# Carry by 128 channels, a second buffer and a later normalisation in a state-space scan on GpSimd and VectorE

## The chip, the cores and the metric

The kernel runs on one core of one Trainium2 chip. The metric is the device time of one execution in microseconds; the median of the runs is compared. Engine names in the profile: PE is TensorE (PEld its weight loads), DVE VectorE, ACT ScalarE, POOL GpSimd, SP SyncE; SPq is SyncE's queue, from which every DMA of the stage is issued.

## The reference

A network of two layers on x of shape 4 x 128 x 64 x 64, in fp32. Layer 0 (convolutions, an ordering of patches and a scan with 16 states) is not touched. Layer 1 takes the 4096 tokens of each batch (128 features), normalises them, and adds this scan with 256 states for each of 256 channels:

```
x_proj = x @ W_in;  xs, z = split(x_proj)
delta = xs @ W_delta;  Bv = xs @ W_B;  Cv = xs @ W_C
state = exp(delta_t[d] * A[d, n]) * state + delta_t[d] * B_t[n] * xs_t[n]
y_t[d] = sum over n of state[d, n] * C_t[n]
out = (y * silu(z)) @ W_out
```

The n-th state is fed by the n-th channel of xs, so B times xs is one vector over n, called `u` in the kernel. After a second normalisation the layer adds a spectral filter: sixteen causal convolutions over all 4096 tokens, each followed by a 128 x 128 matrix, two versions of each (for the sequence and for the sequence with alternating signs), and three short taps.

## The kernel before

Layer 1 is one loop over 8192 steps in an order written out by hand. A part is a chunk of 512 tokens of one batch: 4 batches x 8 chunks are 32 parts of 256 steps, and step d of a part does channel d for all 256 states (two halves of 128 partitions) and 512 tokens. `normalise`, `project`, `output`, `fetch`, `carry`, `spread`, `lift`, `scan`, `contract` and `put` are functions inside `layer1`.

What is issued at step k, in this order:

- `fetch` (L1068), every second step: one DMA `dlb<-delta` (L1071) brings the deltas of channels k+8 and k+9, 512 tokens each, to all partitions. Four such buffers.
- `carry` (L1074): in parts after a batch's first chunk, two GpSimd instructions (L1079, L1080) multiply the factors of the first token, `af`, by the states kept in `last`, and add the result to the first values `vf`. Now 32 channels at a time, six steps ahead of the first of them.
- `spread` (L1082), every second step, four ahead: one GpSimd instruction (L1085) multiplies `u` by the deltas of two channels for tokens 1 to 511 and both halves, 2044 elements per partition, into one of three buffers `v`; a small ScalarE copy (L1089) puts the first token's `vf` beside it.
- `lift` (L1092), one ahead: two ScalarE activations (L1094) write exp(delta A) into one of two PSUM buffers `da`.
- jobs that are due (`later`), then one piece of the block product's work: after each eight channels, `contract` (L1102) splits into six pieces: TensorE products `yp` (L1114), the ScalarE copies `ye` of `put` (L1120) with a DMA `yd<-ye` (L1121), and the copy to `last` (L1125).
- `scan` (L1096): one VectorE instruction (L1097), 1024 elements, reading `da` and `v`.
- a piece of the side work `beside(n)`: `output` of the part before, then `project` of the part after. Both are generators that yield "mm" (taken at step 6 of each eight), "post" (step 7) or "free" (the next step). Each contains one `normalise` (L744): statistics on VectorE, two small ScalarE instructions, a power and a product on GpSimd (L759, L760), then four ScalarE activations (L764). The last piece of `project` is the Exp of `af`. The last of `output` stores `x3` and, for every second chunk, hands over a block of 1024 tokens to the spectral filter.
- at step 7 of each eight, `fetch_y` issues four or eight small DMAs `yt<-yd` (L1137).
- matrix products of the spectral filter, `conv` (L1045) and `fin` (L989), as many columns as a step's credit allows (1.4 x 512 at first, 1.7 x 512 from the middle of the third batch). Their inputs are loaded up to three products ahead by `load` (L948): `pq` (L956, five buffers) and `strip` (L962, three buffers), by SyncE. What is left when the steps are over is issued after the loop.

Every engine executes its own instructions in that order, and so does SyncE's queue: a DMA that waits for a buffer holds all DMAs behind it.

Of the kernel before, what the change touches and what calls it, by code (L numbers as in the profile page):

```python
# [8 lines left out]
F32 = mybir.dt.float32  # L9
# [588 lines left out]
GD = 8  # L598
# [78 lines left out]
def layer1(ctx: ExitStack, tc, ident, half, w_in, w_delta, w_b, w_c, w_out, a_t, phi, pqd, mud, x2, x3, out):  # L677
# [20 lines left out]
    wk = ctx.enter_context(tc.tile_pool(name="s_wk", bufs=2))  # L698
    sp = ctx.enter_context(tc.tile_pool(name="s_sp", bufs=3))
# [44 lines left out]
    def normalise(t):  # L744

        st = sm.tile([128, NT, 6], F32, tag="st", name="st")
        mv = sm.tile([128, NT, 2], F32, tag="mv", name="mv")
        for i in range(NT):
            nc.vector.bn_stats(st[:, i, :], t[:, i, :])
        for i in range(NT):  # L750
            nc.vector.bn_aggr(mv[:, i, :], st[:, i, :])
        yield "free"
        ve = sm.tile([128, NT], F32, tag="ve", name="ve")
        nc.scalar.activation(ve, mv[:, :, 1], AF.Identity, bias=eps)
        ms = sm.tile([128, NT], F32, tag="ms", name="ms")
        nc.scalar.activation(ms, mv[:, :, 0], AF.Copy, scale=-1.0)
        yield "free"
        rs = sm.tile([128, NT], F32, tag="rs", name="rs")
        nc.gpsimd.tensor_tensor(rs, ve, half[:, :NT], ALU.pow)  # L759
        nc.gpsimd.tensor_tensor(ms, ms, rs, ALU.mult)  # L760
        yield "free"
        yield "free"
        for i in range(NT):
            nc.scalar.activation(  # L764
                t[:, i, :], t[:, i, :], AF.Identity, bias=ms[:, i : i + 1], scale=rs[:, i : i + 1]
            )
# [11 lines left out]
    def project(b, ch, into):  # L778
# [12 lines left out]
        yield "free"  # L791
        tr = tr.rearrange("p (i c) -> p i c", i=NT)
        yield from normalise(tr)
        yield "mm"
        ps = middle()
# [152 lines left out]
    def load(i):  # L948

        (b, blk, sources, _, _), r, k, side, src = queue[i]
        if src == sources[0]:
            segs = (0, 2) if blk == 0 else (min(blk + 1, 3), 1)
            pq = sp.tile([128, 2, 128], F32, tag="pq", name="pq", bufs=5)
            nc.sync.dma_start(pq[:, 0 : segs[1]], pqd[k, side][:, bass.ds(*segs)])  # L956
            mats[i] = pq
        lo = max(0, 512 * (blk - src) - 384)
        width = 896 if src < blk else 512
        strip = sp.tile([128, 896], F32, tag="strip", name="strip")  # L960
        start = (NK + k) * row + r if side else k * row + 1
        nc.sync.dma_start(strip[:, :width], bass.AP(phi.tensor, start + lo, [[1, 128], [1, width]]))  # L962
        strips[i] = strip, lo

    def products():
# [50 lines left out]
        while True:  # L1016
# [15 lines left out]
            while issued < len(queue) and issued < i + 3:  # L1032
                load(issued)
                issued += 1
# [33 lines left out]
    def fetch(d, ready):  # L1068

        dl = wk.tile([128, VD, TS], F32, tag="dlb", name="dlb", bufs=4)  # L1070
        nc.sync.dma_start(dl, ready[3][bass.ds(d, VD), :].partition_broadcast(128))  # L1071
        return dl

    def carry(ch, d, ready):  # L1074

        af, vf = ready[4:]
        cols = bass.ds(d, 32)
        if ch:
            nc.gpsimd.tensor_tensor(af[:, :, cols], af[:, :, cols], last[:, :, cols], ALU.mult)  # L1079
            nc.gpsimd.tensor_tensor(vf[:, :, cols], vf[:, :, cols], af[:, :, cols], ALU.add)  # L1080

    def spread(d, dl, ready):  # L1082

        v = wk.tile([128, VD, 2, TS], F32, tag="v", name="v", bufs=3)
        nc.gpsimd.tensor_tensor(  # L1085
            v[:, :, :, 1:], ready[0][:, :, 1:].unsqueeze(1).broadcast_to((128, VD, 2, TS - 1)),
            dl[:, :, 1:].unsqueeze(2).broadcast_to((128, VD, 2, TS - 1)), ALU.mult,
        )
        nc.scalar.copy(v[:, :, :, 0], ready[5][:, :, bass.ds(d, VD)].rearrange("p h d -> p d h"))  # L1089
        return v  # L1090

    def lift(d, da, dl):  # L1092
        for h in range(2):
            nc.scalar.activation(da[:, h, 1:], dl[:, d % VD, 1:], AF.Exp, scale=at[:, h, d : d + 1])  # L1094

    def scan(d, s, v, da):  # L1096
        nc.vector.tensor_tensor_scan(  # L1097
            s[:, d % GD].rearrange("p h t -> p (h t)"), da.rearrange("p h t -> p (h t)"),
            v[:, d % VD].rearrange("p h t -> p (h t)"), 0.0, ALU.mult, ALU.add,
        )  # L1100

    def contract(s, c, g, keep):  # L1102


        yd = dr.tile([130, NT, 32, GD], F32, tag="yd", name="yd", bufs=12)
        yp = {}

        def products(i):
            if i % 2 == 0:
                yp[i // 2] = pm.tile([128, 2, GD, 32], F32, tag="mm", name="yp")  # L1110
            for h in range(2):
                for q in range(4):
                    t = bass.ds(128 * i + 32 * q, 32)
                    nc.tensor.matmul(  # L1114
                        yp[i // 2][bass.ts(q, 32), i % 2], c[:, h, t], s[:, :, h, t], start=h == 0, stop=h == 1
                    )

        def put(j):
            ye = wk.tile([128, 2, 32, GD], F32, tag="ye", name="ye", bufs=1)
            nc.scalar.copy(ye, yp[j].rearrange("p i d t -> p i t d"))  # L1120
            nc.sync.dma_start(yd[0:128, 2 * j : 2 * j + 2], ye)  # L1121

        def carried():
            if keep:
                nc.scalar.copy(  # L1125
                    last[:, :, bass.ts(g, GD)].rearrange("p h d -> p d h"), s[:, :, :, TS - 1]
                )

        def take(yt):

            flat = yd.rearrange("p i t d -> (p i t d)")
            for q in range(4):
                rows = flat[bass.ds(32 * q * NT * 32 * GD, 32 * (NT * 32 + 1) * GD)]
                rows = rows.rearrange("(r x) -> r x", r=32)[:, 0 : NT * 32 * GD].rearrange(
                    "r (i y) -> r i y", i=NT
                )[:, :, 0:GD]
                nc.sync.dma_start(yt[bass.ts(q, 32), :, bass.ts(g, GD)], rows)  # L1137

        return [
            lambda: products(0), lambda: products(1), lambda: put(0), lambda: products(2),  # L1140
            lambda: (products(3), carried()), lambda: put(1),
        ], take

    def due():
        for job in [j for j in later if j[0] <= now[0]]:
            later.remove(job)
            job[2]()
# [6 lines left out]
    steps = 256 * len(parts)  # L1154
# [5 lines left out]
    def beside(n):  # L1160

        if n:
            yield from output(*parts[n - 1], done.pop(n - 1), ready.pop(n - 1)[2])
        if n + 1 < len(parts):
            ready[n + 1] = tiles()
            yield from project(*parts[n + 1], ready[n + 1])
# [9 lines left out]
                    done[m] = big.tile([128, NT, 256], F32, tag="yt", name="yt", bufs=1)  # L1176
                take(done[m])

    for k in range(-8, steps):
        now[0] = k  # L1180
        j = k + 8
        if 0 <= j < steps and j % VD == 0:
            dls[j // VD] = fetch(j % 256, ready[j // 256])
        j = k + 6
        if 0 <= j < steps and j % 32 == 0:
            carry(parts[j // 256][1], j % 256, ready[j // 256])
        j = k + 4
        if 0 <= j < steps and j % VD == 0:
            vs[j // VD] = spread(j % 256, dls[j // VD], ready[j // 256])
        j = k + 1  # L1190
        if 0 <= j < steps:
            lift(j % 256, factors[j % 2], dls[j // VD])
        if k < 0:
            continue
        due()
        n, d = divmod(k, 256)
        b, ch = parts[n]
        if pieces:
            pieces.pop(0)()
        if d % GD == 0:  # L1200
            s = wk.tile([128, GD, 2, TS], F32, tag="s", name="s")
        scan(d, s, vs[k // VD], factors[k % 2])
        if d % GD == GD - 1:
            more, take = contract(s, ready[n][1], d // GD, ch + 1 < NCH)
            pieces += more
            takes.append((n, take))
        if d == GD:
            side = beside(n)
            kind = next(side, None)
        at_step = d % GD  # L1210
        if kind == "free" or (kind == "mm" and at_step == 6) or (kind == "post" and at_step == 7):
            kind = next(side, None)
        if at_step == GD - 1:
            fetch_y(n, d)
        pace = 1.4 if n < 5 * NCH // 2 else 1.7
        credit = min(credit + pace * TS, pace * TS)
        while credit > 0:
            cost = next(spectral)
            if cost == 0:
                break  # L1220
            credit -= cost
# [93 lines left out]
```

## Time and profile before

| | us |
|---|---|
| median of 3 runs | 22132.84 (22130.33 to 22134.94) |
| the profiled execution's own time | 22129.28 |
| its span, first to last instruction | 22127.6 |
| VectorE busy | 20448.7 (92%) |
| GpSimd busy | 20181.7 (91%) |
| TensorE busy (matmuls) | 17758.9 (80%) |
| ScalarE busy | 15725.0 (71%) |

The span holds layer 0 and the weights of the spectral filter (up to about 3140 us), the 256-state stage (first spread at 3142.1, last scan at 21771.5) and a rest in which the spectral filter ends. A row of a group gives line, engine, operation, the tiles written and read, count, then the busy time and the mean duration in ns, then the engine's idle time just before these instructions and what ended it. A row of waits gives who waited for whom, us in total, times and the longest. A row of a timeline gives the start and the length in us.

### The profile page before, as it was taken

The page shows a single profiled execution, that of the slowest core. Times are in us where ns is not written, and L with a number is a line of the kernel's source. Part 1 is how long each engine was busy: PE and PEld are TensorE (multiplying, and loading weights), DVE is VectorE, ACT ScalarE, POOL GpSimd, SP SyncE. Part 2 cuts the span into 40 slices and gives each one's busy share as a digit, 9 for nine tenths or more (in the row PEclk, how much of TensorE's full clock was granted, in tenths as well). Part 3 has the DMA queues.
Part 4 walks back from the last instruction along what each step waited for, and adds up shares of the span by engine and source line. Part 5 has one row for each costly group of instructions (what it writes and reads, how often), then busy time and mean ns, then how long its engine had stood idle before and what let it go on. Part 6 is the DMA issues. An engine that isn't in the chain of part 4 may idle for free.

```text
span 22127.6 us, 292872 instructions
## 1 busy us (share of the span) xinstructions
PE 17758.9 (80%) x99156; PEld 7777.4 (35%) x99156; DVE 20448.7 (92%) x11842; ACT 15725.0 (71%) x28971; POOL 20181.7 (91%) x5932
## 2 busy tenths in 40 slices
PE   8788844474867888886858888869598899999999
PEld 4444421131323333342323333324233344434344
DVE  3588879999999999999999999999999999999993
ACT  0477747777777777777777777777777777777773
POOL 0477759999999999999999999999999999999993
PEclk9899976686988999997979999979699999999999
DMA  0255544464656776675656777757577677777775
GB/s 27 78 139 140 140 136 151 150 198 151 206 186 200 218 222 218 218 220 180 213 173 217 220 219 218 220 179 229 164 225 222 216 233 233 232 230 230 230 226 154
DMA packets 2399971, 4238.15 MB, mean 192 GB/s; under 512 B 778200, under 2 KB 1235968, under 8 KB 2395136
## 3 DMA queue, kind: packets, MB, share of 16 engines
q1 hardware_dynamic: 2398464, 4219.40, 62.0%
q8 instruction: 781, 12.80, 0.2%
q14 instruction: 726, 5.95, 0.1%
HBM read 3600.52 MB, written 617.88 MB: 191 GB/s over the span
## 4 chain that ended last, share of the span: by engine, by line
DVE 49%; POOL 17%; PE 14%; ACT 9%; issue 6%; DMA 4%; SPq 0%; DVEq 0%; POOLq 0%; ACTq 0%
DVE s L1097 43%; POOL v L1085 16%; ACT da L1094 6%; PE conv L1045 6%; DVE states L493 3%; PE conv L96 2%; DMA yd<-ye 2%; PE yp L1114 2%; DVE p L497 2%; PE fin L989 1%; ACT f L485 1%; PE y L509 1%; PE mm L402 0%; ACT t L764 0%; ACT ye L1120 0%
## 5 line engine op out<-in xcount | busy, mean ns | idle before, releaser
L1085 POOL TENSOR_TENSOR v<-u,dlb 128x2044 f32<-128x2044 f32 x4096 | 18343.1, 4522 | 111.5 <-DMA dlb<-delta 93.7
L1097 DVE TENSOR_TENSOR_SCAN s<-da,v 128x1024 f32<-128x1024 f32 x8192 | 18056.5, 2270 | 383.3 <-ACT da L1094 315.7
L1094 ACT ACTIVATE da<-dlb,at 128x511 f32<-128x511 f32 x16384 | 11299.4, 690 | 2062.9 <-DVE s L1097 1598.3
L1045 PE MATMUL conv<-strip,tok 128*128 128x512 f32 (+3 forms) x20480 | 8646.5, 552 | 3.9 <-DMA strip<-in_phi 3.8
L1114 PE MATMUL yp<-s,c 128*32 128x256 f32 x65536 | 5015.4, 437 | 2972.2 <-DVE s L1097 1617.2
L1045 PEld LDWEIGHTS conv<-strip,tok 128*128 128x128 f32 x20480 | 3689.4, 192 | 4132.0 <-issue 3754.7
L1114 PEld LDWEIGHTS yp<-s,c 128*32 128x32 f32 x65536 | 1987.9, 121 | 6755.1 <-issue 1831.8
L1089 ACT COPY v<-vf 128x4 f32<-128x4 f32 x4096 | 813.4, 199 | 2260.8 <-DVE s L1097 2142.4
L471 POOL TENSOR_TENSOR v<-dx,bcb 128x1024 f32<-128x1024 f32 x512 | 1207.2, 2358 | 433.4 <-DVE states L493 427.9
L989 PE MATMUL fin<-conved,pq 128*128 128x512 f32 (+1 forms) x3200 | 1423.1, 540 | 13.5 <-ACT conved L1056 4.2
L493 DVE TENSOR_TENSOR_SCAN states<-f,v 128x1024 f32<-128x1024 f32 x512 | 1176.0, 2297 | 172.5 <-ACT f L485 123.3
L1120 ACT COPY ye<-yp 128x512 f32<-128x512 f32 x2048 | 1186.1, 579 | 148.9 <-DMA yd<-ye 132.2
L485 ACT ACTIVATE f<-dt,an 128x255 f32<-128x255 f32 x2048 | 973.4, 476 | 418.7 <-DVE states L493 368.0
L509 PE MATMUL y<-p,ident 128*128 128x512 f32 x2048 | 1005.1, 619 | 149.4 <-DVE p L497 144.4
L1056 ACT COPY conved<-conv 128x512 f32<-128x512 f32 x1344 | 778.2, 579 | 338.3 <-PE conv L1045 336.8
L497 DVE TENSOR_TENSOR p<-states,bcb 128x1024 f32<-128x1024 f32 x512 | 627.1, 1225 | 41.1 <-DVE states L493 2.7
L989 PEld LDWEIGHTS fin<-conved,pq 128*128 128x128 f32 x3200 | 532.0, 194 | 226.0 <-issue 164.1
L509 PEld LDWEIGHTS y<-p,ident 128*128 128x128 f32 x2048 | 368.4, 195 | 680.4 <-issue 355.2
L127 POOL TENSOR_TENSOR rs<-sq,half 128x1 f32<-128x1 f32 x4 | 2.2, 560 | 485.2 <-DVE sq L125 485.2
L402 PE MATMUL mm<-ow,yg 128*32 128x128 f32 x2048 | 283.2, 298 | 106.8 <-ACT om L406 105.3
L402 PEld LDWEIGHTS mm<-ow,yg 128*32 128x32 f32 x2048 | 236.8, 139 | 213.6 <-ACT om L406 128.4
L1005 DVE TENSOR_TENSOR xo<-xo,fin 128x512 f32<-128x512 f32 x32 | 21.3, 665 | 300.8 <-PE fin L997 300.8
(232 smaller groups left out, 6259.3 us busy)
## 6 DMA issues: line engine op xcount, KB each, us to landing
dlb<-delta SPq DMA_DIRECT2D x4096, 512.0 KB, 4.1
strip<-in_phi SPq DMA_DIRECT2D x1536, 448.0 KB, 4.7
yd<-ye SPq DMA_DIRECT2D x2048, 256.0 KB, 4.0
bcb<-bcd SPq DMA_DIRECT2D x1024, 256.0 KB, 4.2
strip<-in_phi SPq DMA_DIRECT2D x1024, 256.0 KB, 4.3
pq<-pqd SPq DMA_DIRECT2D x1088, 64.0 KB, 3.9
yt<-yd SPq DMA_DIRECT2D x4096, 4.0 KB, 3.3
pq<-pqd SPq DMA_DIRECT2D x256, 128.0 KB, 4.0
```

Of the source, the lines that this page charges most:

```text
L471: nc.gpsimd.tensor_tensor(v, ready[n][2][:, :, bass.ts(i, SUB)].unsqueeze(1).broadcast_to((128, 2, 2, SUB)), bc[:, 0].unsqueeze(2).broadca ...
L485: nc.scalar.activation(factors[j % 2][:, a, k, 1:], ready[n][1][:, k, SUB * i + 1 : SUB * i + SUB], AF.Exp, scale=an[:, k, 2 * g + a : 2 * ...
L493: nc.vector.tensor_tensor_scan(states.rearrange(flat), factors[j % 2].rearrange(flat), v.rearrange(flat), 0.0, ALU.mult, ALU.add)
L497: nc.vector.tensor_tensor(p, states, bc[:, 1].unsqueeze(2).broadcast_to((128, 2, 2, SUB)), ALU.mult)
L509: nc.tensor.matmul(t.rearrange("p k t -> p (k t)"), ident, p[:, a].rearrange("p k t -> p (k t)"), start=g == 0 and a == 0, stop=False, ski ...
L989: nc.tensor.matmul(fin[:, bass.ds(c0, w)], pq[:, n, :], u[:, bass.ds(c0, w)], start=begin and n == 0, stop=end and not partly, skip_group_ ...
L1045: nc.tensor.matmul(ps[:, skip:], tok[:, 1 - r if side else r, j, :], strip[:, bass.ds(c0 - lo, TS - skip)], start=src == sources[0] and j ...
L1085: nc.gpsimd.tensor_tensor(v[:, :, :, 1:], ready[0][:, :, 1:].unsqueeze(1).broadcast_to((128, VD, 2, TS - 1)), dl[:, :, 1:].unsqueeze(2).br ...
L1094: nc.scalar.activation(da[:, h, 1:], dl[:, d % VD, 1:], AF.Exp, scale=at[:, h, d : d + 1])
L1097: nc.vector.tensor_tensor_scan(s[:, d % GD].rearrange("p h t -> p (h t)"), da.rearrange("p h t -> p (h t)"), v[:, d % VD].rearrange("p h t ...
L1114: nc.tensor.matmul(yp[i // 2][bass.ts(q, 32), i % 2], c[:, h, t], s[:, :, h, t], start=h == 0, stop=h == 1)
L1120: nc.scalar.copy(ye, yp[j].rearrange("p i d t -> p i t d"))
```

## The change

Three edits in the 256-state stage. `carry` takes 128 channels in one pair of instructions and is issued ten steps ahead of the first of them; the loop therefore begins two steps earlier. `ye` has the pool's two buffers in place of one, and `pq` four in place of five. In `normalise` five pieces lie between the GpSimd power and the activations, in place of two.

```diff
@@ normalise
         nc.gpsimd.tensor_tensor(rs, ve, half[:, :NT], ALU.pow)
         nc.gpsimd.tensor_tensor(ms, ms, rs, ALU.mult)
-        yield "free"
-        yield "free"
+        for _ in range(5):
+            yield "free"
         for i in range(NT):
@@ load
-            pq = sp.tile([128, 2, 128], F32, tag="pq", name="pq", bufs=5)
+            pq = sp.tile([128, 2, 128], F32, tag="pq", name="pq", bufs=4)
@@ carry
-        cols = bass.ds(d, 32)
+        cols = bass.ds(d, 128)
         if ch:
             nc.gpsimd.tensor_tensor(af[:, :, cols], af[:, :, cols], last[:, :, cols], ALU.mult)
             nc.gpsimd.tensor_tensor(vf[:, :, cols], vf[:, :, cols], af[:, :, cols], ALU.add)
@@ put
-            ye = wk.tile([128, 2, 32, GD], F32, tag="ye", name="ye", bufs=1)
+            ye = wk.tile([128, 2, 32, GD], F32, tag="ye", name="ye")
@@ the loop over steps
-    for k in range(-8, steps):
+    for k in range(-10, steps):
...
-        j = k + 6
-        if 0 <= j < steps and j % 32 == 0:
+        j = k + 10
+        if 0 <= j < steps and j % 128 == 0:
             carry(parts[j // 256][1], j % 256, ready[j // 256])
```

## The prediction

> **What bounds the kernel now.** I read the page's groups of instructions first: two groups of nearly the same size fill two engines.
>
> ```profile
> L1085 POOL TENSOR_TENSOR v<-u,dlb 128x2044 f32<-128x2044 f32 x4096 | 18343.1, 4522 | 111.5 <-DMA dlb<-delta 93.7
> L1097 DVE TENSOR_TENSOR_SCAN s<-da,v 128x1024 f32<-128x1024 f32 x8192 | 18056.5, 2270 | 383.3 <-ACT da L1094 315.7
> ```
>
> A spread on GpSimd serves two scans on VectorE, 4.52 us against 2 x 2.27. So the busy times over the 256-state stage alone decide (the windows view; columns: window, length, then busy us of PE, PEld, DVE, ACT and POOL, clock, DMA share, GB/s):
>
> ```profile
> 3146.00:21774.00 18628.00, 14902.14 (x90440) 6340.33 (x90444) 18243.90 (x9028) 13984.76 (x25818) 18533.51 (x4668) 0.90 0.66 207
> 21774.00:22127.60 353.60, 344.98 (x1060) 179.39 (x1052) 5.29 (x14) 62.31 (x111) 1.22 (x2) 1.00 0.41 116
> ```
>
> GpSimd is busy 18,533.5 of 18,628 us, 99.5%; VectorE has 384 us to spare. The stage is a GpSimd queue with small holes; the last 354 us are TensorE's (345 busy). The waits of the stage, VectorE's, then ScalarE's, then SyncE's queue (total us, times, longest):
>
> ```profile
> DVE s L1097 <- ACT da L1094: 315.7, 173, 5.3
> DVE s L1097 <- POOL v L1085: 58.3, 95, 7.8
> ```
>
> ```profile
> ACT ye L1120 <- DMA yd<-ye: 130.0, 89, 6.2
> ACT v L1089 <- POOL vf L1080: 112.4, 94, 1.4
> ACT t L764 <- POOL ms L760: 110.3, 51, 3.2
> ```
>
> ```profile
> SPq L1071 <- ACT da L1094: 8420.5, 3632, 5.7
> ...
> SPq L962 <- PE conv L1045: 560.4, 458, 4.9
> ```
>
> The reader is to see that ScalarE's three waits (353 us) resemble VectorE's 316 us: ScalarE stalls, the next factor `da` is late, the scan waits. But VectorE catches up, since GpSimd is slower; such a stall costs time only where it reaches GpSimd. It does so by one route, seen in the timeline:
>
> ```profile
> 4404.76 1.65 ACT L764 ACTIVATE t<-t,ms,rs 128x128 f32<-128x128 f32 x4 [2.99 <-POOL ms L760]
> ...
> 4407.81 17.56 DVE L1097 TENSOR_TENSOR_SCAN s<-da,v 128x1024 f32<-128x1024 f32 x8 [3.42 <-ACT da L1094]
> ...
> 4463.64 4.50 POOL L1085 TENSOR_TENSOR v<-u,dlb 128x2044 f32<-128x2044 f32 x1 [4.65 <-DMA dlb<-delta]
> ```
>
> A `dlb` load reuses a buffer that `lift` still reads, so SyncE issues it only when ScalarE has passed. With ScalarE and VectorE 3 us late, and a burst of eight `yt` loads (3.76 us on SyncE from 4449.30) and six `pq` and strip loads ahead of it, the load went out at 4456.02 and GpSimd stood 4.65 us. GpSimd's waits for `dlb` come to 93.7 us in 19 times; 44.2 of them are one, before the stage's first spread. That leaves 49.5 us in 18, and with the other idle before spreads (111.5 - 93.7 = 17.8) some 67 us in the loop.
>
> **What the Trainium skill says.** GPSIMD Engine Reference, section 3.1: a `tensor_tensor` of 2048 fp32 takes 4497 ns on GpSimd and pays a software dispatch per instruction. The trace agrees: 4522 ns at 2044 elements, 332 at 64. Perfetto Trace Analysis, Optimization Strategy: the same gap repeating on the engine that should be saturated can mean too few buffers. Here it half agrees: the one `ye` buffer stalls ScalarE (130 us), not the saturated engine. DMA: Bandwidth & Descriptors, Anatomy of one DMA: the semaphore wait of a DMA is served on the issuing sequencer before dispatch. The SyncE rows agree: 8,420 us of such waits, and everything later stands behind each.
>
> **The change part by part.**
>
> *Carry.* Now 8 pairs in each of 28 chunks:
>
> ```profile
> L1079 POOL TENSOR_TENSOR af<-af,last 128x64 f32<-128x64 f32 x224 | 74.5, 332 | 0.0
> L1080 POOL TENSOR_TENSOR vf<-vf,af 128x64 f32<-128x64 f32 x224 | 71.4, 319 | 17.6
> ```
>
> ```profile
> 9999.01 40.23 POOL L1085 TENSOR_TENSOR v<-u,dlb 128x2044 f32<-128x2044 f32 x9
> 10039.20 0.32 POOL L1079 TENSOR_TENSOR af<-af,last 128x64 f32<-128x64 f32 x1
> 10039.60 0.32 POOL L1080 TENSOR_TENSOR vf<-vf,af 128x64 f32<-128x64 f32 x1
> 10039.87 4.49 POOL L1085 TENSOR_TENSOR v<-u,dlb 128x2044 f32<-128x2044 f32 x1
> ```
>
> Nine spreads end at 10039.24 and the next starts at 10039.87; neighbours otherwise overlap by some 0.05 us (4522 ns long, 40.23/9 = 4.47 apart). A pair costs 0.68 us; 224 cost 152 us. Afterwards there are 56 pairs of 128x256. Between 64 and 2044 elements one costs (4522 - 332)/1980 = 2.12 ns, so each instruction grows by 192 x 2.12 = 407 ns and a pair costs 0.68 + 0.81 = 1.49 us; 56 cost 83. **Saved 69 us**, all on the saturated queue. Bounds: a quarter more per pair leaves 48, a quarter less gives 90.
>
> *Carry ten steps ahead.* It moves past three spreads instead of one in GpSimd's queue, so ScalarE's copy L1089 finds it done; 112 us of ScalarE's waiting go. For the next chunk it now stands at step 246; the Exp of `af` it needs is issued near step 184 and moves 16 later: covered.
>
> *Normalisation.* The four activations L764 come five steps after the GpSimd power instead of two; the 110 us go. The instructions stay. Everything behind a normalisation moves one group of eight steps (its "mm" slot recurs every eight): the output's rest by 8, the projection by 16. Its `delta` and `gate` stores, the next `x` load and the `pq` and strip loads of a new block move with it on SyncE; at the new place there are again eight `yt` loads, so the burst stays.
>
> *That shift has a price.* A block's products enter the queue 8 steps later and, where it had run dry, start later. In the order of the two programs' TensorE instructions, 198,656 columns of products stand after the last block product now, 205,312 then: 13 products of 512 columns. In the tail such a product takes 0.86 us (two passes 0.43 apart in the timeline): **lost 11 us**. The bounds are 10 and 12 (353.6 us over 388 products).
>
> *ye.* 130 us of ScalarE's waiting go; next late there is `yp`. No instruction is added.
>
> *pq, 5 to 4.* This adds a wait. With a single source per product (704 of 1,344 loads, counted from the tasks), the `pq` load of product m waited for `fin` of m-5, which ends before the `conv` of m-3 that the strip load behind it waits for; now it waits for `fin` of m-4, which is after. Each such strip, and what stands behind it on SyncE, goes out about 0.86 + 0.4 = 1.3 us later. I take nothing for it: SyncE waits 2.3 us on average (8,420/3,632) ahead of the `dlb` loads. In the tail a strip has two products and a `fin`, 6.9 us, and lands in 3.3. Bounds: none, or the third rival.
>
> *What ScalarE's waits give back.* Chunks with stalls lose up to 3 us of lateness ahead of the burst, so each of the 18 waits (mean 2.75 us) shrinks by up to 3. I take 67 down to about 22: **saved 45 us**. Bounds: 0 and 67. Longer carries do not open new waits: VectorE needs 18,567 us with all of today's stalls (18,243.9 busy, 315.7, 7.6 on others) and far less without them, GpSimd 18,628 - 69 - 45 = 18,514.
>
> Sum against the profiled execution's own 22,129.3 us: -69 - 45 + 11 = -103, 22,026. The median of the runs stands 3.5 us above that execution, so **22,030 us**.
>
> **The rivals.** (1) The waits for `dlb` stay, because the burst itself makes them: -69 + 11, 22,075. For it: the burst is as long as before. Against it: the 3 us of lateness that precede it. (2) VectorE becomes the bound because ScalarE's stalls only change their name: then the stage ends at VectorE's 18,567 and a few us, 58 less than now; with the tail 22,086. For it: margins of under 1%. Against it: only 53 of its 316 us of waits (18,567 - 18,514) need go for GpSimd to stay the bound, and 353 us of ScalarE's causes are removed. (3) Slower: the `pq` wait. 704 x 1.3 = 915 us of delay on SyncE; if a quarter reaches the spreads through `dlb`, 229 us, and nothing of the 45 is gained: 22,133 - 69 + 11 + 229 = 22,304. It decides once more than about 11% reaches them (69 + 45 - 11 = 103 us). For it: SyncE is already held 560 us by `conv` in the stage. Against it: the slack ahead of `dlb`. That the carry would not get shorter is excluded by the program: 112 instructions of 128x256 in place of 448.
>
> **How the numbers follow.** About 0.2% (44 us) is what a measurement of this kernel tells from no change. Forecast 0.70, rival 1 0.15, rival 2 0.09, rival 3 0.06. The forecast's own bounds (carry 48 to 90, waits 20 to 65) give some 22,000 to 22,060; rival 1 ends at 22,075 and rival 2 at 22,086, so the range is 22,000 to 22,085. Rival 2 straddles the bound and goes half to no change: faster 0.88, same 0.06, slower 0.06.
>
> **What would show it.** L1079 and L1080 with 56 instructions each of about 0.73 us; the stage some 114 us shorter and the last scan near 21,658 us; the tail near 365 us; ScalarE's waits L1120 on `yd`, L1089 on `vf` and L764 on `ms` near nothing; VectorE's wait for `da` below 200 us and for `v` above 58; GpSimd's wait for `dlb` near 65 (44 of it the first). SyncE's L956 waits for `fin` rise from tens to hundreds of us. The forecast is wrong if a carry pair moves the next spread by over 2 us, if the waits for `dlb` rise, or if GpSimd falls below 99% of the stage.

## The result, and the profile after

The median fell from 22,131.6 us (22,129.6 to 22,134.9, 4 runs) to 22,030.9 us (22,028.3 to 22,034.0, 4 runs): ratio 0.9954, 95% interval 0.9937 to 0.9972, some 101 us. The profiled execution has a span of 22,032.3 us.

The page's two large groups, after the change:

```profile
L1085 POOL TENSOR_TENSOR v<-u,dlb 128x2044 f32<-128x2044 f32 x4096 | 18333.9, 4533 | 69.2 <-DMA dlb<-delta 65.5
L1097 DVE TENSOR_TENSOR_SCAN s<-da,v 128x1024 f32<-128x1024 f32 x8192 | 18133.3, 2272 | 192.6 <-ACT da L1094 90.7
```

GpSimd's idle time before spreads fell from 111.5 to 69.2 us, VectorE's before scans from 383.3 to 192.6, and these are different things: the first is on the path, the second mostly not. The windows of the stage and of the rest (columns as before):

```profile
3146.00:21664.00 18518.00, 14862.66 (x90422) 6331.34 (x90426) 18321.05 (x9028) 13988.77 (x25817) 18478.42 (x4332) 0.90 0.67 208
21664.00:22032.30 368.30, 358.38 (x1082) 185.56 (x1074) 5.29 (x14) 64.17 (x114) 1.22 (x2) 0.99 0.41 115
```

The stage is 110 us shorter (18,628 to 18,518; counted from the first spread, which came 2.1 us later in this execution, 112), the rest 15 longer (353.6 to 368.3). GpSimd is busy 99.8% of the stage: it is still the bound, with fewer holes. GpSimd's groups of the carry in the stage:

```profile
L1079 POOL TENSOR_TENSOR af<-af,last 128x256 f32<-128x256 f32 x56 | 42.3, 755 | 0.0
L1080 POOL TENSOR_TENSOR vf<-vf,af 128x256 f32<-128x256 f32 x56 | 40.7, 726 | 4.4
```

The waits of the stage, GpSimd's, VectorE's, then SyncE's:

```profile
POOL v L1085 <- DMA dlb<-delta: 65.5, 10, 44.0
POOL v L1085 <- DVE s L1097: 3.7, 2, 3.5
```

```profile
DVE s L1097 <- ACT da L1094: 90.7, 57, 3.3
DVE s L1097 <- POOL v L1085: 86.6, 83, 7.8
```

```profile
SPq L962 <- PE conv L1045: 482.4, 397, 4.4
...
SPq L956 <- PE fin L989: 210.1, 164, 4.7
```

Of the 65.5 us the first wait, ahead of the stage, is again 44.0. So 21.5 us in nine waits are left of 49.5 in 18. GpSimd's wait for VectorE, which holds the `v` buffers, fell from 11.3 to 3.7. ScalarE's three waits have left its list: none of L1120 for `yd`, of L1089 for `vf` or of L764 for `ms` in the stage. VectorE now waits about as long for GpSimd as for ScalarE, as it should beside a saturated GpSimd. SyncE's wait for `fin`, 17.5 us before, is 210; its wait for `conv` fell from 560 to 482, so the sum grew by 115.

What is left of the holes has the same picture as before, eight steps later in a part (timelines of SyncE's queue and of GpSimd):

```profile
4464.53 4.78 SPq L1137 DMA_DIRECT2D yt<-yd  x8
...
4472.27 1.02 SPq L1071 DMA_DIRECT2D dlb<-delta  x2
```

```profile
4480.03 4.51 POOL L1085 TENSOR_TENSOR v<-u,dlb 128x2044 f32<-128x2044 f32 x1 [4.51 <-DMA dlb<-delta]
```

The burst of eight `yt` loads and six loads of a new block is still in front of the `dlb` load; the lateness ahead of it is gone, so only some parts still meet it.

### The profile page after: what moved, and what is told of

The parts are those of the page before. It is cut to its first block, busy times and chain, and to the rows that moved or that the text cites. A ratio compares the mean times of both kernels' runs of the same rounds, so it can differ in the third digit from the quotient of the medians.

```text
span 22032.3 us, 292179 instructions
## 1 busy us (share of the span) xinstructions
PE 17738.9 (81%) x99156; PEld 7780.4 (35%) x99156; DVE 20525.7 (93%) x11842; ACT 15730.0 (71%) x28971; POOL 20124.5 (91%) x5596
## 4 chain that ended last, share of the span: by engine, by line
DVE 49%; POOL 23%; PE 11%; ACT 8%; issue 6%; DMA 2%; SPq 0%; DVEq 0%; POOLq 0%; ACTq 0%
DVE s L1097 43%; POOL v L1085 22%; ACT da L1094 5%; PE conv L1045 4%; DVE states L493 3%; PE conv L96 2%; DVE p L497 2%; PE yp L1114 1%; ACT f L485 1%; PE fin L989 1%; DMA dlb<-delta 1%; PE y L509 1%; PE mm L402 1%; DMA yd<-ye 0%; PE ranked L255 0%
## 5 line engine op out<-in xcount | busy, mean ns | idle before, releaser
L1085 POOL TENSOR_TENSOR v<-u,dlb 128x2044 f32<-128x2044 f32 x4096 | 18333.9, 4533 | 69.2 <-DMA dlb<-delta 65.5
L1097 DVE TENSOR_TENSOR_SCAN s<-da,v 128x1024 f32<-128x1024 f32 x8192 | 18133.3, 2272 | 192.6 <-ACT da L1094 90.7
L1089 ACT COPY v<-vf 128x4 f32<-128x4 f32 x4096 | 812.6, 198 | 2239.1 <-DVE s L1097 2236.4
L1120 ACT COPY ye<-yp 128x512 f32<-128x512 f32 x2048 | 1185.0, 579 | 11.7 <-PE yp L1114 10.4
```

Of the source, the lines that this page charges most:

```text
L1085: nc.gpsimd.tensor_tensor(v[:, :, :, 1:], ready[0][:, :, 1:].unsqueeze(1).broadcast_to((128, VD, 2, TS - 1)), dl[:, :, 1:].unsqueeze(2).br ...
L1097: nc.vector.tensor_tensor_scan(s[:, d % GD].rearrange("p h t -> p (h t)"), da.rearrange("p h t -> p (h t)"), v[:, d % VD].rearrange("p h t ...
```

## The experiments

**Carry alone (e1_carry_only).**

```diff
-    for k in range(-8, steps):
+    for k in range(-10, steps):
-        j = k + 6
-        if 0 <= j < steps and j % 32 == 0:
+        j = k + 10
+        if 0 <= j < steps and j % 128 == 0:
-        cols = bass.ds(d, 32)
+        cols = bass.ds(d, 128)
```

> The carry edit alone (128 channels, ten steps ahead), normalisation and buffers as before. Theory A, GpSimd's queue is the stage: 168 pairs fewer and 56 longer ones give 70 us, about 22,062 us; GpSimd's waits for dlb in the loop stay near 50 us, since ScalarE still waits for ms (about 110 us) and for yd (about 130 us); TensorE's tail stays near 354 us. Theory B, ScalarE's stalls pace the stage and the gain is shared out by them (130 : 112 : 110 of some 115 us): only the wait for vf goes, 37 us, about 22,095 us.

Measured: 22,088.1 us against 22,131.2, ratio 0.998 (0.9971 to 0.9988): 43 us, between the two theories and nearer to B's 22,095. GpSimd's waits in its stage and its window:

```profile
POOL v L1085 <- DMA dlb<-delta: 59.4, 20, 6.1
POOL v L1085 <- DVE s L1097: 20.7, 30, 4.8
```

```profile
3146.00:21731.00 18585.00, 14907.09 (x90440) 6334.36 (x90444) 18224.41 (x9028) 13986.27 (x25818) 18478.53 (x4331) 0.90 0.67 208
```

GpSimd's busy time is that of the full change (18,478.5 us, 55 below the kernel before; another 13 are the gaps of 0.08 us inside the 168 pairs that no longer exist). But its idle time before spreads is 92.6 us by its group, where the kernel before had 111.5 - 44.2 = 67.3: 25 us of the saving came back as longer waits. Both kinds of waits grew: for `dlb` from 49.5 to 59.4, for VectorE from 11.3 to 20.7. With shorter carries VectorE has less time to catch up after each stall of ScalarE; the waits for `ms` (94.8 us) and for `yd` (129.5) are still there. The amount is measured; this reading of it is an inference until the runs below.

**Normalisation alone (e2_norm_only).**

```diff
-        yield "free"
-        yield "free"
+        for _ in range(5):
+            yield "free"
```

> The later normalisation alone (five pieces for two), carry and buffers as before. Theory A: GpSimd's own work is unchanged; its waits for dlb in the loop fall from 50 us to about 25, its other idle a little, 30 to 40 us in all, and the tail grows by 11 to 15 us: about 22,106 us (22,100 to 22,115). Theory B: 36 us gained, 15 lost in the tail, about 22,110 us; this run does not tell the two apart by its time, only by whether GpSimd's waits for dlb are what shrank.

Measured: 22,099.0 us, ratio 0.9986 (0.9979 to 0.9993), 32 us, 1 us below the range that theory A gave. GpSimd's wait, then the window of the rest:

```profile
POOL v L1085 <- DMA dlb<-delta: 69.2, 11, 44.1
```

```profile
21735.50:22103.50 368.00, 358.69 (x1086) 185.53 (x1086) 5.29 (x14) 64.28 (x114) 1.22 (x2) 0.99 0.41 115
```

25 us of waits in the loop are left in place of 49.5, with GpSimd's own work unchanged, and the tail is that of the full change: this edit alone makes both. ScalarE still waits 175 us for `vf` and 117 for `yd` here.

**Buffers alone (e3_buffers_only) and the carry's place alone (e4_carry_place_only).**

```diff
# e3_buffers_only
-            ye = wk.tile([128, 2, 32, GD], F32, tag="ye", name="ye", bufs=1)
+            ye = wk.tile([128, 2, 32, GD], F32, tag="ye", name="ye")
-            pq = sp.tile([128, 2, 128], F32, tag="pq", name="pq", bufs=5)
+            pq = sp.tile([128, 2, 128], F32, tag="pq", name="pq", bufs=4)
# e4_carry_place_only
-    for k in range(-8, steps):
+    for k in range(-10, steps):
-        j = k + 6
+        j = k + 10
```

> Only the buffers: ye two for one, pq four for five. Theory A: ScalarE's 130 us of waiting for yd go but do not reach GpSimd, since they come after the burst's worst point: 0 to 10 us gained, 22,122 to 22,132 us. Theory B: 42 us gained, about 22,090 us. Rival of the pq wait: slower by 20 us or more, with GpSimd's waits for dlb well above 94 us.

> The carry stays 32 channels wide (224 pairs of 128x64) but is issued ten steps ahead instead of six. Theory A: ScalarE's wait for vf (112 us) goes, GpSimd's work does not change, so the time stays within 10 us of before, about 22,128 us. Theory B: 37 us gained, about 22,095 us.

Measured: buffers 22,121.9 us, ratio 0.9995 (0.9987 to 1.0004); place 22,129.3 us, ratio 1.0 (0.9991 to 1.0008). Each took a wait of over 110 us off ScalarE (130 for `yd`, 112 for `vf`) and gave 9 and 2 us, neither clear of its interval; theory B asked for 42 and 37. All twelve runs with the buffers lie below the median of the kernel before, so some of the 9 us may be real.

Neither run is a clean count. With two `ye` buffers the wait for `ms` rose from 110 to 147 us. With the carry earlier GpSimd waited less for `dlb` (28.5 us in the loop, 49.5 before) but more for VectorE (26.3, 11.3 before), and that profile is of the fastest of its twelve executions, 8 us below their median. Still, removing a wait of ScalarE does not shorten the kernel by a share of its length: theory B's prices are refuted.

**Carry and normalisation together (e11_carry_and_norm).** The kernel before with the edits of e1 and e2:

```diff
-        yield "free"
-        yield "free"
+        for _ in range(5):
+            yield "free"
...
-        cols = bass.ds(d, 32)
+        cols = bass.ds(d, 128)
...
-        if 0 <= j < steps and j % 32 == 0:
+        if 0 <= j < steps and j % 128 == 0:
```

> The carry and normalisation edits together, the buffers of the kernel before (ye one, pq five). Against e7_ye_one it differs only by pq five for four. Theory A, the pq wait is absorbed on SyncE: the same time within 6 us, about 22,036 us, GpSimd's waits for dlb near 70 us (44 of them the first). Rival of the pq wait: it has a price that e7_ye_one and the changed kernel carry; then this run is faster than e7_ye_one by 15 us or more, under 22,023 us. It also says whether carry and normalisation add up: alone they gave 43 and 32 us; if the 27 us that the carry alone lost to longer dlb waits come back once ScalarE's wait for ms is gone, together they give about 95, not 75.

Measured: 22,036.2 us against 22,133.1, ratio 0.9955 (0.9938 to 0.9972): 97 us, where the two alone sum to 75. The intervals are too wide to tell 97 from 75; the profile does it:

```profile
POOL v L1085 <- DMA dlb<-delta: 27.5, 11, 4.8
POOL v L1085 <- DVE s L1097: 0.5, 1, 0.5
```

With the waits for `ms` gone, GpSimd waits 27.5 us for `dlb` in the loop and 0.5 for VectorE, in place of e1's 59.4 and 20.7. From its first scan to its last the stage is 106 us shorter than before, where e1's and e2's are 42 and 41: the carry's lost part comes back. So these two edits must be priced together.

**One ye buffer again (e7_ye_one).**

```diff
-            ye = wk.tile([128, 2, 32, GD], F32, tag="ye", name="ye")
+            ye = wk.tile([128, 2, 32, GD], F32, tag="ye", name="ye", bufs=1)
```

> The changed kernel with one ye buffer again (pq stays at four). Theory A, a stall of ScalarE costs time only where it reaches GpSimd through a late dlb load: ScalarE waits some 120 us for yd again, GpSimd's waits for dlb grow by under 15 us, about 22,040 us (22,031 to 22,046). Theory B, every stall counts by its length: about 22,070 us or more.

Measured: 22,038.2 us, 7 above the changed kernel, though ScalarE waits 147 us for `yd` again. VectorE's wait:

```profile
DVE s L1097 <- ACT da L1094: 176.0, 116, 5.0
```

This is the cleaner test of theory B, which asked for 22,070 us or more: VectorE waits 85 us longer for `da` than in the changed kernel, but GpSimd's waits for `dlb` in the loop grow by 6 us only (69.9 - 42.2 = 27.7 against 21.5). From e11 it differs only by `pq` four for five: 2 us, within the runs of either. The `pq` wait has no price that can be measured at four. Five buffers of `pq` beside two of `ye` were not run.

**Three pq buffers (e6_pq_three).**

```diff
-            pq = sp.tile([128, 2, 128], F32, tag="pq", name="pq", bufs=4)
+            pq = sp.tile([128, 2, 128], F32, tag="pq", name="pq", bufs=3)
```

> The changed kernel with pq three instead of four: the load of a single-source product now waits for a fin that stands behind the next product's conv, so SyncE is held for about a whole product (3.0 us in the tail, more in the paced loop) in place of one fin. Theory A, SyncE's slack ahead of the dlb loads absorbs most of it in the loop; in the tail the strip then has one product and two fins, 3.9 us, for a load that lands in 3.3: about 22,060 us (22,035 to 22,110), GpSimd's waits for dlb 70 to 130 us. Rival, every us of SyncE's delay reaches the spreads by a quarter or more: 22,300 us or more.

Measured: 22,227.9 us, ratio to the kernel before 1.0042 (1.0027 to 1.0057), 197 us above the changed kernel; the expectation was far too low. SyncE's wait in the stage, then GpSimd's (the first one lies ahead of this window):

```profile
SPq L956 <- PE fin L989: 1918.2, 622, 9.9
```

```profile
POOL v L1085 <- DMA dlb<-delta: 151.2, 108, 4.7
```

One buffer fewer turns 210 us of SyncE's waiting into 1,918. I had set it against the average slack ahead of the `dlb` loads, 2.3 us; single waits are up to 9.9 us long. Of the 1,708 us added, 130 (151.2 - 21.5) show up on GpSimd, 8%, not a quarter. Where they sit, by the same view from 18,230 us on, about the start of part 26 (counted from 0):

```profile
POOL v L1085 <- DMA dlb<-delta: 114.0, 89, 4.5
```

Three quarters of the 151.2 us fall in these last six parts, where most products have a single source. The rest of the loss is TensorE: the time after the last scan is 431 us instead of 369, and 33.3 us in it are `conv` waiting for strips. So the third rival's mechanism exists, and one buffer fewer than the changed kernel has brings it out.

**Three pieces, and the power one piece earlier (e5_norm_three, e9_pow_earlier).** Both start from the changed kernel and keep the matmul slot.

```diff
# e5_norm_three
-        for _ in range(5):
+        for _ in range(3):
# e9_pow_earlier
         nc.scalar.activation(ms, mv[:, :, 0], AF.Copy, scale=-1.0)
-        yield "free"
         rs = sm.tile([128, NT], F32, tag="rs", name="rs")
...
-        for _ in range(5):
+        for _ in range(4):
```

> The changed kernel with three pieces between power and activations instead of five: the activations then come one step later than in the kernel before and the next matmul slot is not missed, so 198,656 columns of products are left for the tail as before. Theory A: the tail goes back to 354 us (15 less than in the changed kernel), ScalarE's wait for ms falls from 110 us to under 30 (one step is 2.2 us, the longest wait was 3.2), GpSimd's waits for dlb in the loop come to 25 to 40 us: about 22,022 us (22,012 to 22,035). Rival: only the whole five steps free ScalarE; the waits for ms stay near 80 us, those for dlb near 60, and the time is 22,050 us or more.

> The changed kernel with GpSimd's power and product issued one piece earlier (in the same piece as the two ScalarE instructions before them) and four pieces after it: the activations stand four steps behind the power, and no matmul slot is missed. Theory A: ScalarE's wait for ms is near nothing, the tail is 354 us as before, GpSimd's waits for dlb in the loop are about 25 us as in the changed kernel: about 22,016 us (22,010 to 22,024). Rival: GpSimd waits for ScalarE's ve and the gain is lost, 22,030 us or more.

Measured: 22,022.4 us both, ratios 0.995 (0.9935 to 0.9965) and 0.995 (0.9934 to 0.9967), 8.5 below the changed kernel. The window of e9's rest:

```profile
21663.00:22018.60 355.60, 346.67 (x1060) 180.17 (x1052) 5.29 (x14) 62.41 (x111) 1.22 (x2) 1.00 0.42 115
```

The tail is 12.7 us shorter than the changed kernel's and the products in it are 13 fewer, so the shift by a group is what lengthened it. Three pieces, one more than before, left ScalarE 20.8 us of waiting for `ms` in e5; four left none in e9's stage, with no difference in time.

**The yt loads in two fours (e10_yt_spread).** From e9:

```diff
-        for _ in range(2):
-            if takes and takes[0][0] <= n - 1 or d >= 6 * GD and len(takes) > 1:
+        early = d % GD == 3
+        for i in range(1 if early else 2):
+            if takes and not early and takes[0][0] <= n - 1 or d >= 6 * GD and len(takes) > 1 and not i:
...
-        if at_step == GD - 1:
+        if at_step == GD - 1 or at_step == 3:
             fetch_y(n, d)
```

> As e9_pow_earlier, and the eight yt loads that stand together at step 7 of a group of eight (from channel 48 on) are issued four at step 3 and four at step 7: the same loads, half the burst (1.9 us of SyncE's queue instead of 3.8). If the burst makes what is left of GpSimd's waits for dlb, they fall from about 25 us in the loop to under 12, about 22,003 us. If only the lateness of ScalarE and VectorE makes them, they stay near 25 us and the time is that of e9_pow_earlier, about 22,016 us.

Measured: 22,006.4 us, ratio 0.9942 (0.9928 to 0.9957), 16 below e9. GpSimd's wait:

```profile
POOL v L1084 <- DMA dlb<-delta: 54.6, 7, 44.3
```

10 us are left in the loop where e9 had 26 (69.5 - 43.8). The burst, then, makes most of what is left: rival 1 of the prediction was right about the remainder. This is the fastest of the complete kernels, some 25 us below the changed one.

**Without the carry (e12_no_carry).** From e10; the states of a chunk are then not carried into the next, so this kernel does not compute the whole result:

```diff
     def carry(ch, d, ready):
-        af, vf = ready[4:]
-        cols = bass.ds(d, 128)
-        if ch:
-            nc.gpsimd.tensor_tensor(af[:, :, cols], af[:, :, cols], last[:, :, cols], ALU.mult)
-            nc.gpsimd.tensor_tensor(vf[:, :, cols], vf[:, :, cols], af[:, :, cols], ALU.add)
+        return
```

> e10_yt_spread with the carry left out (the states of a chunk are not carried into the next, so part of the computation is missing). It takes the last 112 carry instructions off GpSimd. Theory A: 56 pairs of 1.5 us, 84 us, less what longer waits for dlb and for v slots give back (carry alone gave back 27 of 70): 21,925 to 21,950 us. Rival, VectorE has by now become the bound of the stage (busy 18,330 of 18,506 us by its group): less than 40 us gained, 21,965 us or more.

Measured: 21,922.3 us, ratio 0.9904 (0.9889 to 0.9919), 84 us below e10: 1.50 us for each of 56 pairs, all of it. Its stage:

```profile
3146.00:21563.00 18417.00, 14861.82 (x90448) 6313.48 (x90452) 18264.47 (x9028) 13988.56 (x25818) 18398.62 (x4219) 0.90 0.68 209
```

GpSimd, at 99.9%, is the bound even here. Its idle time before spreads fell too, from 12 us in e10's loop to 8. Where VectorE's lateness does not reach GpSimd (VectorE still waits 116 us for `da` here), a microsecond off GpSimd is a microsecond off the kernel; that is the other side of e1.

## Why the prediction was right

*The bound.* GpSimd's queue was to be the stage. e12 (the full 84 us), e7 (7 us for 147 us of ScalarE's waits), e3 and e4 show it; rival 2 falls. That ScalarE's 353 us of waits resemble VectorE's 316 was no account of them: VectorE still waited 289 us for `da` without the waits for `yd` (e3) and 305 without those for `vf` (e4), but 167 without those for `ms` (e2). Once those are gone, one `ye` buffer adds 85 us to VectorE's wait (e7), and still hardly any time.

*Carry, 69 us.* The instructions took 755 and 726 ns against 738 and 725 worked out from the slope, and e12 puts a pair at 1.50 us against 1.49. The term was right on the queue. But the sum let it stand by itself; alone it gave 43 us. It needs the normalisation's edit, which the prediction listed as a separate gain; its "longer carries do not open new waits" does not hold for the carry alone.

*Waits for dlb, 67 us to about 22, 45 saved.* Measured 67.3 to 25.2 (69.2 - 44.0): 42 saved. The size was right, the way to it only in part. The prediction let each of the 18 waits shrink; instead half of them went and the nine that stayed are about as long as before (2.4 us each, 2.75 before). And 28 of the 42 us are waits for `dlb`; the other 14 are other idle time before spreads (17.8 to 3.7), 7.6 of it waits for a `v` buffer that VectorE still held. This is a second route by which lateness reaches GpSimd, where the prediction named one. That the wait for `ms` is the lateness that counts is shown by e2, which alone brings 67 down to 28 us (24 of it off `dlb`) while the waits for `vf` and `yd` go on, and by e11; `vf` and `yd` have little part (e4, e3, e7). The split between lateness and burst, only argued beforehand, is e10's: about 16 of the remaining 26 us were the burst of `yt`.

*Tail, 11 us lost.* Measured 15 in the one profile, 12.7 against e9, whose products match the kernel before. The changed kernel, e2, e7 and e11, all with five pieces, have tails of 368.0 to 369.3 us; the kernel before, e1, e5, e9 and e10 have 353.6 to 356.7. The columns of the two programs were the right quantity; the price per product was low, 0.98 us (12.7/13) instead of 0.86, and outside the bounds of 10 to 12. What the other 0.12 us are is open.

*pq at nothing.* Right at four (e11 against e7, 2 us). The price put on rival 3, 915 us of delay on SyncE, was far too high: SyncE's waits for `fin` and `conv` together grew by 115 us. Its share of a quarter was too high too; 8% was measured at three buffers. Yet with three it decides, by 1,708 us of delay and by the tail.

*ye at nothing of its own.* 7 to 9 us (e7, e3), in the same direction but not clear of the interval in e3.

The sum, -69 - 45 + 11 = -103, reads -68 (224 x 0.68 less 56 x 1.50), -42, +15 and +2 for a later first spread by the profiles, -93, where the two spans differ by 95 and the medians by 101. The waits and the tail were sized 3 and 4 us too well. That the median lies within 1 us of the forecast is therefore partly luck: one execution differs from the next by some 5 us here.

## What to carry to other kernels

When two engines run at nearly the same pace, ask which one's idle time is small in its own view, and price every stall by the route on which it reaches that engine; here over 350 us of waits on ScalarE had a price only where they reached GpSimd, by a late `dlb` load or by a `v` buffer that VectorE still held. A saving on the saturated queue also takes away the pauses in which its partner catches up, so cut the partner's stalls in the same change. Where side work has fixed slots, count in the order of the two programs what a delay makes it miss: three pieces instead of five gave nearly the same cover (28 us of idle time before spreads against 25) without the lost slot.

## What the hardware showed that was not expected

SyncE's queue, which only issues DMAs here, was tolerant up to a point and then not: its wait for a matrix buffer went from 17.5 us (five buffers) to 210 (four; 230 in e3, where only buffers were changed) without a measurable price, and to 1,918 (three) at a price of 197 us, of which TensorE's tail took some 62. GpSimd's elementwise time was linear enough to be interpolated: 755 and 726 ns for 256 elements against 738 and 725 from 64 and 2044.
